# Projections two blocks at a time in the first layer of a four-layer kernel

## The chip, the cores and the metric

The kernel runs on one core of one Trainium2 chip. The metric is device time in microseconds (us) of one execution. A core has a matrix engine (PE; PEld are its weight loads), a vector engine (DVE), a scalar engine (ACT), a general engine (POOL), and a queue (SP) that issues transfers (DMA) between the chip's memory and the on-chip buffers. In the trace of this kernel each engine works off its instructions in the order of its program, and so does SP; they wait for each other through semaphores.

## The reference

The network has four layers on an image batch of 2 x 512 channels x 64 x 64 pixels, all float32. Each layer normalises its input by groups and adds its result to it. Only the first layer matters here. Cut down:

```python
xf = x.reshape(B, C, N).transpose(0, 2, 1)                 # N = 4096 pixels, C = 512
q  = xf @ W_q + b_q                                         # 8 heads of 64 channels
kv = xf @ W_kv + b_kv
k_l, v_l = kv[..., :C], kv[..., C:]
q_norm, k_l = l2norm(q), l2norm(k_l)                        # by head
q_scaled = (q_norm + query_embedding) * softplus(temperature)
# each pixel attends to its 3 x 3 neighbours and to 256 pooled tokens
attn_local = einsum(q_scaled, 9 shifted copies of k_l)
attn_pool  = einsum(q_scaled, l2norm(k_pool))
attn = softmax(concat(attn_local, attn_pool))
lt = einsum(q_norm, learnable_tokens) + learnable_bias + a_local
x_local = sum over 9 neighbours of lt * shifted v_l
x_pool  = a_pool @ v_pool
out = (x_local + x_pool) @ W_proj + b_proj
```

## The kernel before

For each of the two images the four layers run one after the other. The first layer is the class `Local`. It works in 16 units: a unit is one chunk of 128 channels (two heads) by 1,024 pixels, which are two blocks of 512 pixels, `j = 0` and `j = 1`. The loop in `run` is a software pipeline: in the iteration of unit u the following stages run side by side, a step of each in turn (`in_turn`), ten or eleven steps in all:

- `projections`: queries for unit u + 3, keys for u + 4 and values for u + 1. One projection of one block is `project` (L133): four accumulating matmuls of 128 x 128 weights with 128 x 512 data into one PSUM bank. ACT then takes it out of PSUM (L2004 and L2006, with the squares for the norm; L2110 for values).
- `norms` and `normed` (L2036, L2043, the small operations of L2050 to L2058, L2064, L2078, L2086): the l2 norms, of the four streams that the iteration before projected. `learned` is L2099.
- `tap_products` (L2126): DVE multiplies the queries of unit u + 1 with the nine shifted copies of the keys, through three buffers. `tap_sums` (L2139) adds these products up over the channels by matmuls 32 columns wide, two for each neighbour.
- `attend` of unit u: scores against the pooled tokens (L2171, two heads, called four times), exponentials on ACT (L2175), values (L2181), sums of the exponentials on POOL (L2186), denominators (L2193, L2197), their reciprocal on DVE (L2218) and the local weights (L2221, L2222). These weights go to a buffer in memory, `rows` (L2225), from which they are fetched again, spread over 128 partitions, as "taps" (`fetch_tap`, L2235).
- `weigh` of unit u - 1: L2248 and L2251, and then for each of the nine taps two copies on ACT (L2258), two products with the values on DVE (L2261) and one addition on POOL (L2265). A tap is two transfers. There are three tap buffers, so tap k + 3 is fetched after tap k has been added. At the end the sum goes to memory (`yd`, L2271), for the output projection (L1966) that comes later.

The matmuls write to PSUM, of which this stage has eight banks: five that rotate among all of these (`mm`), one for the sums of taps, two for the queries. The code says the order of work only roughly. The tile framework puts the instructions of the whole program in an order of its own for each engine, and the SP queue, when the program is built. The order that it made for PE in a unit of the steady stage, beginning with the denominators, is:

```
L2193 L2197 | project k1 | L2099 | 5 taps | project q0 | 1 tap | project q1 | L2171 |
project v0 | L2036 | L2171 | L2248 | L2043 | L2181 | 4 taps | L2171 | 1 tap | project v1 |
L2171 | 4 taps | L2064 | L2181 | L2078 (k) | 3 taps | project k0 | L2078 (q)
```

A "tap" here is one matmul of L2139, of which a unit has 18. On the SP queue the order of a steady unit is: two transfers to `rows`, four fetches (taps 0 and 1), the one to `yd`, two fetches (tap 2), and later twelve fetches (taps 3 to 8).

The lines with the projections in the step loop are these, before:

```python
for step in range(10):
    if step >= 6:
        project((uk, uq)[step // 2 - 3], "kq"[step // 2 - 3], step % 2)
    if step % 3 == 0 and values:
        u, j = values.pop(0)
        self.value(u, j)
```

Of the kernel before, what the change touches and what calls it, by code (L numbers as in the profile page):

```python
# [1692 lines left out]
class Local:  # L1693
# [300 lines left out]
    def projections(self, uk, uq, uv, streams):  # L1994

        nc = self.nc

        def project(u, which, j):
            if u is None:
                return  # L2000
            b = self.bias[which][:, u // self.UN:][:, :1]
            ps = self.projected(which, u % self.UN * 2 + j)
            part = self.raw[which][:, j * TB:(j + 1) * TB]
            nc.scalar.activation(part, ps, AF.Identity, bias=b)  # L2004
            sq = self.sq[len(streams)]
            nc.scalar.activation(sq, ps, AF.Square, bias=b)  # L2006
            streams.append((which, u, j, part, sq))
            if j and self.last(u):
                self.fetch(which, u // self.UN + 1)

        last = KC * self.UN - 1
        values = [(uv, 0), (uv, 1)] if uv is not None and uv < last - 1 else []
        if uv == last - 1:

            values = [(u, j) for u in (uv, last) for j in range(2)]
        for step in range(10):
            if step >= 6:
                project((uk, uq)[step // 2 - 3], "kq"[step // 2 - 3], step % 2)
            if step % 3 == 0 and values:
                u, j = values.pop(0)  # L2020
                self.value(u, j)
                if j and self.last(u):
                    self.fetch("v", u // self.UN + 1)
            yield

    def norms(self, streams, ended):
# [407 lines left out]
```

## Time and profile before

| | |
|---|---|
| time, median of 3 runs (lowest, highest) | 5502.16 us (5494.62, 5505.77) |
| span of the profiled run | 5486.4 us |
| PE busy | 5213.3 us (95%) |
| PE weight loads busy | 2263.8 us (41%) |
| DVE busy | 3063.3 us (56%) |
| ACT, POOL busy | 1797.6 us, 1802.6 us (33% each) |
| first layer's units, first image | from about 250 to 1,050 us |
| the same, second image | from about 2,990 to 3,790 us |

PE is the busiest engine by far, but the profile warns that busy PE is not PE at its peak, since its matmuls overlap and their ends are modelled. So the starts of groups of matmuls are what is read from it: the distance from one group's start to the next. In the timeline each float32 matmul appears as two records, so a projection of one block is a row "x8".

### The profile page before, as it was taken

To read this page: it belongs to the slowest core of one execution; us is meant where nothing else is said; L and a number is where in the kernel's file an instruction comes from. 1 tells how busy PE (TensorE), PEld (TensorE's weight loads), DVE (VectorE), ACT (ScalarE), POOL (GpSimd) and SP (SyncE) were. 2 spreads that over 40 slices of the span, in tenths; PEclk is the share of its full clock that TensorE was granted. 3 is DMA by queue.
4 is the path that set the end of the run, shared out by engine and by line. 5 is a ranking of instruction groups with operands and counts; after the bars stand their busy time and mean duration, and the time that the engine had idled before them with its cause. 6 is when DMAs were issued, how large, how long until landed. Compare 5 with 4: busy or idle time off the path is not lost. (4 is left out here: it accounts for less than half of the span.)

```text
span 5486.4 us, 51908 instructions
## 1 busy us (share of the span) xinstructions
PE 5213.3 (95%) x19291; PEld 2263.8 (41%) x19291; DVE 3063.3 (56%) x3804; ACT 1797.6 (33%) x3441; POOL 1802.6 (33%) x1198
## 2 busy tenths in 40 slices
PE   7899999999988899999998999999999889999999
PEld 4333333554333444544343333335543334445443
DVE  3256667745679533544432666676456894334444
ACT  1245555233213233222212555542432222332221
POOL 0025555401310145434400355553013001554443
PEclk9899999999989999999998999999999899999999
DMA  3024445500000000100010344455000000000000
GB/s 140 0 65 126 126 124 157 143 18 24 1 2 0 1 1 8 70 24 31 31 53 0 83 125 127 125 152 148 1 24 1 2 0 1 1 8 16 16 16 24
DMA packets 103354, 276.37 MB, mean 50 GB/s; under 512 B 15090, under 2 KB 28146, under 8 KB 101044
## 3 DMA queue, kind: packets, MB, share of 16 engines
q1 hardware_dynamic: 103092, 272.97, 17.2%
q8 instruction: 154, 2.52, 0.2%
q14 instruction: 108, 0.88, 0.1%
HBM read 224.68 MB, written 48.23 MB: 50 GB/s over the span
## 5 line engine op out<-in xcount | busy, mean ns | idle before, releaser
L133 PE MATMUL mm<-big,w 128*128 128x512 f32 x2560 | 1191.1, 610 | 5.2 <-DVE late L2218 5.1
L133 PEld LDWEIGHTS mm<-big,w 128*128 128x128 f32 x2560 | 468.2, 192 | 695.6 <-issue 594.9
L2265 POOL TENSOR_TENSOR late<-late,big 128x1024 f32<-128x1024 f32 x192 | 454.6, 2368 | 300.7 <-DVE big L2261 298.3
L1265 POOL TENSOR_TENSOR total<-prob 128x512 f32<-128x512 f32 x128 | 159.6, 1270 | 758.8 <-ACT prob L1262 758.8
L1617 POOL TENSOR_SCALAR qf_sum<-qf,ksum_ratio 128x512 f32<-128x512 f32 x128 | 198.9, 1562 | 552.6 <-ACT qf L1667 351.3
L1182 PE MATMUL acc<-big,dg 128*128 128x512 f32 x704 | 319.6, 612 | 56.7 <-DVE big L697 25.6
L1438 POOL TENSOR_TENSOR big<-big 128x512 f32<-128x512 f32 x224 | 277.5, 1270 | 235.4 <-ACT big L1429 235.4
L2186 POOL TENSOR_TENSOR late<-late 128x512 f32<-128x512 f32 x128 | 160.6, 1276 | 510.3 <-ACT late L2175 485.0
L1642 DVE RECIPROCAL k<-psD 128x512 f32<-128x512 f32 x64 | 214.9, 3357 | 185.0 <-PE psD L1639 185.0
L697 DVE TENSOR_TENSOR big<-big 128x3968 f32<-128x3968 f32 x72 | 308.8, 4289 | 6.9 <-DVE big L697 0.9
L2261 DVE TENSOR_TENSOR big<-big,mm 128x512 f32<-128x512 f32 x384 | 254.5, 680 | 71.4 <-ACT mm L2258 68.4
L1429 ACT ACTIVATE big<-mm,ed 128x256 f32<-128x256 f32 x512 | 193.7, 488 | 276.7 <-DVE top L1425 249.0
L2258 ACT COPY mm<-big 128x512 f32<-128x512 f32 x384 | 221.3, 594 | 152.3 <-DMA big<-rows 122.2
L1363 PE MATMUL mm<-proj,k 64*128 64x256 f32 x2048 | 265.2, 391 | 0.9 <-ACT k L1330 0.9
L1282 DVE RECIPROCAL recip<-psD 128x512 f32<-128x512 f32 x64 | 214.9, 3358 | 87.1 <-PE psD L1279 87.1
L2126 DVE TENSOR_TENSOR prod<-qs,big 128x1024 f32<-128x1024 f32 x192 | 230.9, 1218 | 44.9 <-PE tap L2139 42.8
L1262 ACT ACTIVATE prob<-mm 128x512 f32<-128x512 f32 x256 | 132.0, 605 | 364.4 <-PE mm L1259 359.2
L1584 DVE TENSOR_REDUCE tops<-mm 128x2 f32<-128x512 f32 x256 | 159.4, 681 | 163.4 <-PE mm L1363 163.3
L1363 PEld LDWEIGHTS mm<-proj,k 64*128 64x128 f32 x2048 | 207.9, 188 | 94.7 <-issue 78.7
L2265 POOL TENSOR_TENSOR late<-late,tap 128x1024 f32<-128x1024 f32 x96 | 226.6, 2360 | 61.0 <-DVE tap L2261 43.6
L1648 PE MATMUL mm<-k,w 128*128 128x512 f32 x512 | 235.6, 602 | 0.0
L1403 PE MATMUL mm<-w,big 128*128 128x512 f32 x512 | 234.5, 602 | 0.0
(369 smaller groups left out, 8387.7 us busy)
## 6 DMA issues: line engine op xcount, KB each, us to landing
big<-rows SPq DMA_DIRECT2D x384, 256.0 KB, 4.0
tap<-rows SPq DMA_DIRECT2D x192, 256.0 KB, 4.2
yd<-late SPq DMA_DIRECT2D x32, 512.0 KB, 4.2
out<-big SPq DMA_DIRECT2D x64, 256.0 KB, 2.0
big<-in_W_kv SPq DMA_DIRECT2D x8, 1024.0 KB, 6.1
rows<-late SPq DMA_DIRECT2D x64, 128.0 KB, 2.4
big<-yd SPq DMA_DIRECT2D x16, 512.0 KB, 4.5
big<-in_x SPq DMA_DIRECT2D x4, 2048.0 KB, 7.6
```

The costliest lines, as they stand in the source:

```text
L133: self.nc.tensor.matmul(ps, w[:, kc, :], X[:, kc, blk * TB:(blk + 1) * TB], start=(kc == 0), stop=(kc == KC - 1))
L697: nc.vector.tensor_tensor(o, a, b, ALU.max)
L1182: nc.tensor.matmul(accs[b], dg, src[:, b * TB:(b + 1) * TB], start=(j == 0), stop=(j == 6))
L1282: nc.vector.reciprocal(r, psD)
L1363: nc.tensor.matmul(pS[h][i][:, t, :], k[lo:lo + HD, tok:tok + P], proj[lo:lo + HD, :], start=True, stop=True)
L1403: nc.tensor.matmul(ps, X[:, kc, lo:lo + P], wv[:, kc, :], start=(kc == 0), stop=(kc == KC - 1))
L1438: nc.gpsimd.tensor_tensor(a, a, part, ALU.add)
L1648: nc.tensor.matmul(ps, self.wo[:, kc, oc * P:(oc + 1) * P], qs[:, kc, :], start=(kc == 0), stop=(kc == KC - 1))
L2126: self.nc.vector.tensor_tensor(self.prods[k % 3].rearrange("p (y x) -> p y x", x=W), qs, self.kx[:, y + dy:y + dy + self.UY, dx:dx + W], A ...
L2258: nc.scalar.copy(ps, part)
L2261: nc.vector.tensor_tensor(part.rearrange("p (y x) -> p y x", x=W), self.vx[:, y:y + self.UY // 2, dx:dx + W], ps.rearrange("p (y x) -> p y ...
L2265: nc.gpsimd.tensor_tensor(out, out, self.taps[k % 3], ALU.add)
```

## The change

Both blocks of a projection are issued in one step: keys in step 6, queries in step 8 and values in step 2 (before, keys in steps 6 and 7, queries in 8 and 9, values in 0 and 3). In the one iteration that projects the values of the last two units, the second pair comes in step 5. The arithmetic, the tiles and the number of instructions stay as they are. Its purpose is that matmuls of one form follow each other on PE and are less often interleaved with narrower ones.

```diff
         for step in range(10):
-            if step >= 6:
-                project((uk, uq)[step // 2 - 3], "kq"[step // 2 - 3], step % 2)
-            if step % 3 == 0 and values:
-                u, j = values.pop(0)
+
+            if step in (6, 8):
+                for j in range(2):
+                    project((uk, uq)[step // 2 - 3], "kq"[step // 2 - 3], j)
+            for u, j in values[:2] if step in (2, 5) else []:
                 self.value(u, j)
                 if j and self.last(u):
                     self.fetch("v", u // self.UN + 1)
+            if step == 2:
+                values = values[2:]
             yield
```

## The prediction

> **What bounds the kernel now.** I read the page first (busy shares), then the table of windows for single units, then PE's timeline inside a unit, then the timelines of DVE, POOL, SP and ACT at the same place. The page says PE; the windows say that in a steady unit PE has no gap:
>
> ```profile
> PE 5213.3 (95%) x19291; PEld 2263.8 (41%) x19291; DVE 3063.3 (56%) x3804; ACT 1797.6 (33%) x3441; POOL 1802.6 (33%) x1198
> ```
>
> ```profile
> 519.66:565.52 45.86, 45.74 (x165) 14.79 (x165) 31.62 (x51) 25.83 (x45) 26.23 (x13) 1.00 0.48 126
> 565.52:611.38 45.86, 45.74 (x166) 14.79 (x165) 31.61 (x51) 25.88 (x45) 26.21 (x13) 1.00 0.47 127
> ```
>
> A unit takes exactly 45.86 us, PE is busy in 45.74 of them, DVE in 31.6, ACT and POOL in 26. What a group costs is the distance between starts in PE's timeline:
>
> ```profile
> 561.89 3.70 PE L133 MATMUL mm<-big,w 128*128 128x512 f32 x8
> 565.52 1.07 PE L2099 MATMUL mm<-qn,big 128*32 128x512 f32 x8
> ...
> 568.21 3.70 PE L133 MATMUL mm<-big,w 128*128 128x512 f32 x8
> 571.84 1.05 PE L2139 MATMUL tap<-prod,cst 128*32 128x512 f32 x2
> 572.82 3.70 PE L133 MATMUL mm<-big,w 128*128 128x512 f32 x8
> 576.45 1.13 PE L2171 MATMUL mm<-big,kp 64*128 64x512 f32 x4
> ```
>
> A projection takes 3.63 us to the next group; its eight passes alone are 3.43 (in the pooled stage, where projections follow each other, the weight loads of passes start 0.429 apart). So 0.20 is a change of form. A single tap matmul (two passes) costs 0.98; four of them that use the four column strips cost 1.00 together (548.83 to 549.83).
>
> Now the loop that PE hides, with L2193 of this unit at 559.02 as zero:
>
> ```profile
> 562.01 3.37 DVE L2218 RECIPROCAL late<-mm 128x256 f32<-128x256 f32 x2 [0.41 <-PE mm L2197]
> ...
> 568.62 0.68 DVE L2261 TENSOR_TENSOR big<-big,mm 128x512 f32<-128x512 f32 x1
> ```
>
> ```profile
> 569.43 2.36 POOL L2265 TENSOR_TENSOR late<-late,big 128x1024 f32<-128x1024 f32 x1 [5.35 <-DVE big L2261]
> 571.87 2.36 POOL L2265 TENSOR_TENSOR late<-late,tap 128x1024 f32<-128x1024 f32 x1
> ```
>
> ```profile
> 567.33 1.11 SPq L2225 DMA_DIRECT2D rows<-late  x2
> 570.37 2.54 SPq L2235 DMA_DIRECT2D big<-rows  x4
> 574.26 0.33 SPq L2271 DMA_DIRECT2D yd<-late  x1
> ```
>
> The reciprocal starts at 2.99, the last-but-one tap is multiplied at 9.6, POOL adds the last two taps until 15.2, and SP, which had fetched taps 0 and 1 of the next unit at 11.4, then writes `yd`. ACT copies tap 0 only at 584.27 (25.25), some 9 us after it landed. This slack makes PE the only bound.
>
> **What the Trainium skill says.** "TensorEngine Tiling (Array Packing)", section "Tiling Modes": a change of tiling mode drains the array, and tiles of one mode run in parallel. The trace agrees: 0.20 us at each change, and four narrow matmuls for the price of one. "TensorE: Matmul & The Clock Gate", section "Measured speedup vs the span model" and the part before it ("Part 3"): matmuls stay in program order; in the trace too, a group whose data is late holds all after it. "DMA: Bandwidth & Descriptors", section "Anatomy of one DMA": waits for semaphores are at the issuing sequencer, before the transfer is handed over. So a transfer that waits on SP holds those behind it; the SP rows above (`yd` issued 0.03 after POOL's end) fit that.
>
> **The change part by part.** I read the new order of each engine from the built program. A steady unit on PE becomes, from the denominators on:
>
> ```
> L2193 L2197 | L2099 | project q0 q1 | L2171 | L2036 | L2171 | L2248 | 5 taps | L2043 | L2181 |
> 4 taps | project v0 v1 | L2171 | 4 taps | L2171 | 3 taps | L2064 | L2181 | L2078 | 2 taps |
> project k0 k1 | L2078
> ```
>
> 1. Projections: six groups of 3.63 = 21.78 become three of 16 passes, 6.86 + 0.20 = 7.06, = 21.18. Saved 0.60.
> 2. Taps: six pieces (0.98 + 0.99 + 0.98 + 1.00 + 0.99 + 1.81 = 6.75) become five (1.81 + 4 x 1.00 = 5.81). Saved 0.94. L2099 no longer shares its form with taps behind it: 0.12 lost.
> 3. L2043 no longer waits 0.18 for ACT after L2248 (five taps lie between). Saved 0.18.
>
> Sum 1.60: PE's own work is 44.25 a unit. Nothing is added on any engine. What moves is the rest: the whole value projection, some 9 us of PE, has gone from before L2248 to behind tap 0, and the loop above must now close sooner.
>
> 4. The new wait. On SP, `yd` now stands in front of all six fetches of taps 0 to 2. On DVE the product that the fourth of the "4 taps" before v0 needs stands behind the two L2261 of tap 0, as it did before. Step by step from L2193 = 0: the reciprocal at 2.99 lasts to 6.36; then L2261, L2221, L2261 at 0.61 each start at 6.39, 7.0, 7.6, so tap 7 goes to POOL at 8.4 (569.43 - 568.62 = 0.8 later), two additions of 2.4 end at 13.2; `yd` is issued at 13.25, the fetches of tap 0 at 13.6 and 14.2. For their landing unit 12 of the first image, where before has `yd` first too, is the nearest row:
>
> ```profile
> 894.19 0.34 SPq L2271 DMA_DIRECT2D yd<-late  x1
> 894.63 0.38 SPq L1956 DMA_DIRECT2D w<-yd  x1
> 895.17 2.63 SPq L2235 DMA_DIRECT2D big<-rows  x4
> ```
>
> ```profile
> 901.94 1.11 ACT L2258 COPY mm<-big 128x512 f32<-128x512 f32 x2 [2.30 <-DMA big<-rows]
> ```
>
> ```profile
> 904.56 2.16 PE L2171 MATMUL mm<-big,kp 64*128 64x512 f32 x4 [1.27 <-DVE big L2261]
> ```
>
> There it was 7.75 us from `yd`, with another 512 KB in between. At the 230 to 250 GB/s that the transfers show there, those take 2.1; so 5.7, landing at 18.9. Lower bound: the quickest tap lands 3.3 after its issue, at 17.5. Upper: 7.75, at 21.0. From landing: copy and two products to 1.9 later, the product of L2126 1.21, PE goes on at 3.3 after landing = 22.2. PE would be there at 19.4 (19.8, since L2036 waits 0.4 for the squares of q1, now right before it). From there PE has 1.0 (taps) + 23.8 left to the next L2193, and about 0.15 behind a copy on ACT that stands behind v1. Unit: 22.2 + 24.95 = 47.15, which is 1.3 longer than 45.86. Behind the held tap matmul on PE stand the values' projections, both score groups and everything to the next L2193, which restarts the loop; so it is not made up.
>
> 5. Number of units: eleven in each image have both this order and a `yd` before them: 2 x 11 x 1.3 = 28.6. Of the 43 changes of form that go in an image, about ten lie in the ramps: -2 us an image, 4 in all. The last units are bound by DVE, POOL and transfers (before already waits in unit 12, rows above), so I take 0 for them. Other layers are untouched. 5502 + 28.6 - 4 = 5527; I say 5525.
>
> **Rivals.** (A) *PE stays the bound, faster.* Tap 0 lands at 17.5 or DVE and POOL get there earlier; then a unit is 44.25 plus 0.4 for the squares and 0.15: 44.8, 1.06 less: 22 x 1.06 + 4 = 27 less, 5475 (without any wait, 5463). For it: PE busy 45.74 of 45.86, the transfers only half busy (0.48). Against: 17.5 needs the least landing of all. (B) *The two cancel*: landing at 17.6 to 18.1 gives 45.8 to 46.3 a unit, about 5500. (C) *Transfers collide as in unit 12*: landing at 21.0, unit 49.3, +3.4: 5502 + 75 - 4 = 5573. For it: `yd` and six fetches, 2 MB, are then queued at once, and the taps behind `yd` before took a median of 6.1 to land. Against: tap 0 needs only the first half of that.
>
> **How the numbers follow.** Forecast (a new wait, 46.4 to 48 a unit, 5510 to 5545) 0.52; C 0.10; B 0.18; A 0.20. Slower by over 0.2% (above 5513): C and nearly all of the forecast, 0.59. Faster (below 5491): A and a little, 0.22. Same: 0.19. The range leaves out the far half of A and C: 5478 to 5558.
>
> **What would show it.** Right: rows of PE with two projections x16 and 7.06 to the next group; five pieces of taps; `yd` on SP ahead of the taps; ACT's copy of tap 0 waiting for DMA in every unit; PE held about 2 us at the taps before v0, for L2126 (L2129 in the new numbering) or L2261; a unit of 47. Wrong: units of 44.3 to 44.8 with PE full, or the hold at another place.

## The result, and the profile after

The changed kernel takes 5539.57 us (median of 4 runs, 5536.88 to 5544.89) against 5498.39 (4 runs, 5482.31 to 5505.77): a ratio of 1.008, 95% interval 1.0056 to 1.0105. It is slower by 41 us.

First the page's line of busy time. The number of instructions on each engine has not changed, and PE's busy time has grown by 23 us:

```profile
PE 5236.5 (94%) x19291; PEld 2281.3 (41%) x19291; DVE 3064.9 (55%) x3804; ACT 1790.9 (32%) x3441; POOL 1811.8 (33%) x1198
```

The windows of two steady units (length, then busy time of PE, weight loads, DVE, ACT, POOL) put a number on what the page blurs. The unit has grown from 45.86 us to 47.3 and 47.6, and PE now has 1.45 and 1.74 us that no matmul fills:

```profile
671.50:718.80 47.30, 45.85 (x168) 15.15 (x166) 31.76 (x50) 25.52 (x46) 26.57 (x13) 1.00 0.47 122
718.80:766.40 47.60, 45.86 (x168) 15.15 (x166) 31.73 (x50) 25.51 (x46) 26.56 (x13) 1.00 0.47 122
```

PE's timeline of the first of them (start, duration; L2196, the first line of a unit, starts at 671.45). Lines of the changed kernel from L2031 on are three higher than before, so L2142 is a tap sum, L2129 its product on DVE, L2238 a tap fetch:

```profile
675.32 7.13 PE L133 MATMUL mm<-big,w 128*128 128x512 f32 x16
682.38 1.13 PE L2174 MATMUL mm<-big,kp 64*128 64x512 f32 x4
683.44 1.41 PE L2039 MATMUL mm<-sq,cst 128*32 128x512 f32 x8
684.78 1.13 PE L2174 MATMUL mm<-big,kp 64*128 64x512 f32 x4
...
686.90 0.62 PE L2142 MATMUL tap<-big,cst 128*32 128x512 f32 x2
...
691.19 0.62 PE L2142 MATMUL tap<-prod,cst 128*32 128x512 f32 x1
691.19 0.62 PE L2142 MATMUL tap<-big,cst 128*32 128x512 f32 x2
...
693.69 1.05 PE L2142 MATMUL tap<-prod,cst 128*32 128x512 f32 x2 [1.45 <-DVE prod L2129]
694.67 7.13 PE L133 MATMUL mm<-big,w 128*128 128x512 f32 x16
```

Read the starts. The two projections take 7.06 (675.32 to 682.38) where two separate ones took 7.26: the saving is there. But the four tap sums that begin at 691.19 end only at 694.67. That is 3.48 for what costs 1.00, so PE is held (it stands at a matmul whose data is not there) for 2.5 us, and the bracket names a product on DVE.

Which sums these are matters for all that follows. DVE makes nine products for a unit, 0 to 8, and writes them into three buffers in turn, which the trace names `big`, `prod`, `prod`. Each product gives two sums, so the 18 sums can be counted by these names. The five from 686.90 on are sums 1 to 5 (product 0 in `big`, product 1, half of product 2). The four at 691.19 are the second sum of product 2, the two of product 3 in `big`, and the first of product 4: sums 6 to 9. Sum 9 is the one that is held. In the kernel before, sums 6 to 9 begin 35.7 us into the unit and product 4 is done at 32.4; now they begin at 19.7 and it is done at 22.2. The build has brought the sums forward by 16 us and the product by 10.

Now the loop behind it, in the timelines of SP, ACT and DVE:

```profile
680.17 1.10 SPq L2228 DMA_DIRECT2D rows<-late  x2
684.87 0.33 SPq L2274 DMA_DIRECT2D yd<-late  x1
685.37 2.43 SPq L2238 DMA_DIRECT2D big<-rows  x4
```

```profile
690.45 1.11 ACT L2261 COPY mm<-big 128x512 f32<-128x512 f32 x2 [3.42 <-DMA big<-rows]
```

```profile
691.12 1.28 DVE L2264 TENSOR_TENSOR big<-big,mm 128x512 f32<-128x512 f32 x2 [1.70 <-ACT mm L2261]
...
692.43 1.21 DVE L2129 TENSOR_TENSOR prod<-qs,big 128x1024 f32<-128x1024 f32 x1
```

Before, ACT came to tap 0 9 us after it had landed. Now it waits 3.42 us for the landing; DVE waits for ACT, the product that PE needs (692.43) stands on DVE behind the two of L2264 for tap 0, and the whole began when SP stood at `yd` until POOL's last addition ended at 684.84. In the nine units of each image from the third on, the hold is 2.4 to 3.8 us, 2.7 in the median.

Where the 41 us are: in each image, the eleven units from the first L2196 to the twelfth take 521.5 and 521.8 us instead of 503.7 and 503.6, 18 more. The ramp from the norm of the pooled tokens to the first L2196 takes 4.5 and 2.4 more, the stretch behind the twelfth 1.7 more and 2.2 less. Together 42. (The two profiled executions themselves differ by 57, 5543.0 against 5486.4: the other 14 lie outside the first layer, which the change does not touch, and the four times of the kernel before alone are spread over 23.)

### The profile page after: what moved, and what is told of

It is laid out like the page before. It is cut to its first block, busy times and chain, and to the rows that moved or that the text cites. A ratio compares the mean times of both kernels' runs of the same rounds, so it can differ in the third digit from the quotient of the medians.

```text
span 5543.0 us, 51933 instructions
## 1 busy us (share of the span) xinstructions
PE 5236.5 (94%) x19291; PEld 2281.3 (41%) x19291; DVE 3064.9 (55%) x3804; ACT 1790.9 (32%) x3441; POOL 1811.8 (33%) x1198
## 5 line engine op out<-in xcount | busy, mean ns | idle before, releaser
L133 PE MATMUL mm<-big,w 128*128 128x512 f32 x2560 | 1168.5, 606 | 1.7 <-DVE big L2264 1.5
L2264 DVE TENSOR_TENSOR big<-big,mm 128x512 f32<-128x512 f32 x384 | 247.3, 676 | 77.8 <-ACT mm L2261 74.8
L2142 PE MATMUL tap<-prod,cst 128*32 128x512 f32 x768 | 221.6, 614 | 34.1 <-DVE prod L2129 24.7
L2129 DVE TENSOR_TENSOR prod<-qs,big 128x1024 f32<-128x1024 f32 x192 | 230.7, 1215 | 40.6 <-PE tap L2142 38.6
L133 PE MATMUL mm<-big,big 128*128 128x512 f32 x512 | 243.2, 638 | 0.0
```

The lines of the kernel that those rows point to most:

```text
L133: self.nc.tensor.matmul(ps, w[:, kc, :], X[:, kc, blk * TB:(blk + 1) * TB], start=(kc == 0), stop=(kc == KC - 1))
L2129: self.nc.vector.tensor_tensor(self.prods[k % 3].rearrange("p (y x) -> p y x", x=W), qs, self.kx[:, y + dy:y + dy + self.UY, dx:dx + W], A ...
L2142: nc.tensor.matmul(ps[32 * q:32 * q + 32, :], self.cst[:, C_TAPW + 16 - 2 * k:C_TAPW + 48 - 2 * k], self.prods[k % 3][:, j * TB:(j + 1) * ...
L2264: nc.vector.tensor_tensor(part.rearrange("p (y x) -> p y x", x=W), self.vx[:, y:y + self.UY // 2, dx:dx + W], ps.rearrange("p (y x) -> p y ...
```

## The experiments

The theory: PE's own work fell as the prediction says, but PE takes its matmuls in order and now reaches tap sums before their products; these stand on DVE behind work on the taps, and that stands behind `yd` on SP. The rivals: two projections of values in a row hold up the other engines; `yd` ahead of the fetches costs by itself, wherever PE stands; PE's early arrival costs, wherever `yd` stands.

The table has what the traces show, in us from the unit's first matmul: which comes first on SP, when the group with sums 6 to 9 begins, when the product for sum 9 is done, and at which sums PE stands for more than 0.2 us until the product is there. Where units differ, the most common kind is given. Ratios are to runs of the kernel before that were made beside each group of runs, with their 95% interval.

| run | first on SP | sums 6 to 9 begin | product for sum 9 done | PE waits at sum | unit, us | time, us | ratio |
|---|---|---|---|---|---|---|---|
| before | taps 0, 1 | 35.7 | 32.4 | none | 45.86 | 5498.39 | 1 |
| after | `yd` | 19.7 | 22.1 to 23.0 | 9, 15 | 47.2 to 47.7 (most) | 5539.57 | 1.008 [1.0056, 1.0105] |
| keys_only | `yd` | 31.2 | 27.9 | none | 44.83 | 5484.61 | 0.9976 [0.9968, 0.9984] |
| all_values_step0 | `yd` | 30.3 | 30.3 | 11, 13, 15, 17 | 51.4 to 53.3 | 5678.50 | 1.0336 [1.031, 1.0362] |
| all_values_step1 | taps 0, 1 | 30.9 | 30.1 | 11 | 46.05 | 5525.15 | 1.0056 [1.0036, 1.0076] |
| all_values_step3 | taps 0, 1 | 22.4 | 24.4 | 7, 9 | 46.95 to 48.0 (most) | 5543.21 | 1.0085 [1.0059, 1.011] |
| yd_on_act_queue | taps 0, 1 | 31.0, 29.6 in turn | 24.3 to 26.6 | none; 11, 15 in turn | 44.83, 46.33 in turn | 5499.00 | 1.0003 [0.9994, 1.0012] |
| values_only | taps 0, 1 | 34.7 | 27.2 | none | 45.01 | 5485.98 | 0.9973 [0.9963, 0.9983] |
| keys_and_queries | taps 0, 1 | 31.0 | 27.7 | none | 44.63 | 5469.00 | 0.9942 [0.9925, 0.9959] |
| half_yd_on_sp | both, see text | 30.8 | 24.4 to 25.6 | none, see text | 44.60 to 47.1 | 5506.81 | 1.001 [1.0, 1.002] |
| keys_queries_yd_act | taps 0, 1 | 31.0 | 27.7 | none | 44.63 | 5460.49 | 0.9926 [0.9907, 0.9946] |
| keys_queries_values_1_3 | taps 0, 1 | 30.8 | 26.6 | none | 44.41 | 5462.80 | 0.993 [0.9911, 0.9949] |
| keys_and_queries_again | taps 0, 1 | 31.0 | 27.7 | none | 44.63 | 5465.05 | 0.9936 [0.9918, 0.9955] |
| best_values_1_3_yd_act | taps 0, 1 | 30.8 | 26.6 | none | 44.41 | 5460.26 | 0.9926 [0.9912, 0.9939] |

The expectations were written by the place of the sums, "the tap sums behind the first pooled values". That is not enough: only in the changed kernel do sums 6 to 9 stand there. In all the other runs the first sums of a series do, and their products were done by 14.3 us, before any tap had landed. What can be compared from run to run is a sum and its own product.

### keys_only: `yd` first, but sums 6 to 9 come later

```diff
-            if step >= 6:
-                project((uk, uq)[step // 2 - 3], "kq"[step // 2 - 3], step % 2)
+            if step == 6:
+                for j in range(2):
+                    project(uk, "k", j)
+            if step >= 8:
+                project(uq, "q", step % 2)
```

> Only the keys are issued side by side (step 6); queries and values stay as before. In the built order yd stands ahead of all six tap fetches, as in the changed kernel, but value block 0 is still projected before L2248, so PE reaches the tap sums behind the first pooled values about 4 us later than in the changed kernel (near 23.7 us after the denominators, against 22.2 for the data). Theory (the loop over yd, tap fetch, ACT, DVE has become later than PE's arrival): no hold, the unit keeps its savings of 0.2 (one change of form) and 0.8 (taps in six pieces of 5.96 instead of 6.76), 44.9 us, total about 5474, 24 less than before. Rival 'yd ahead of the fetches costs by itself, because 2 MB are queued at once': as the changed kernel, about 5540. Rival 'sixteen passes of the values in a row hold up the other engines': 5474 too.

The unit is 44.83 (44.9 was expected), and the run is 13 us faster than before. In this unit L2196 starts at 523.02. SP writes `yd` and issues tap 0 as late as in the changed kernel (13.41 and 13.90 after it; there 13.42 and 13.92):

```profile
536.43 0.33 SPq L2274 DMA_DIRECT2D yd<-late  x1
536.92 2.42 SPq L2238 DMA_DIRECT2D big<-rows  x4
```

In the timelines of DVE and PE:

```profile
549.73 1.21 DVE L2129 TENSOR_TENSOR prod<-qs,big 128x1024 f32<-128x1024 f32 x1
```

```profile
546.51 0.62 PE L2142 MATMUL tap<-big,cst 128*32 128x512 f32 x2
...
554.23 0.62 PE L2142 MATMUL tap<-prod,cst 128*32 128x512 f32 x1
554.24 0.62 PE L2142 MATMUL tap<-big,cst 128*32 128x512 f32 x2
```

The sums at 546.51 begin with product 0: they are sums 1 to 4, and not those that hold the changed kernel, as the expectation took them to be. Sums 6 to 9 begin at 554.23, 31.2 into the unit, and product 4 (549.73) is done 3.3 us before. So `yd` ahead of the fetches costs nothing in a unit whose sums come that late. What it costs where they come early is not shown by this run. The total fell short of the 24 expected: the eleven units gave 10.6 and 9.9 in the two images, and the ramp took 6.4 and 4.6 of that back.

### yd_on_act_queue: nothing in front of the taps

```diff
-        nc.sync.dma_start(self.yd[:, cc, lo:lo + self.UT], out)
+        nc.scalar.dma_start(self.yd[:, cc, lo:lo + self.UT], out)
```

> The changed kernel with yd issued from ACT's queue instead of SP's, so that nothing stands on SP between the writes to rows and the fetches of taps 0 and 1. The built order of PE then alternates between two patterns, with the values' pair still behind the tap sums that follow the first pooled values. Theory (it is yd in front of the fetches that makes the changed kernel's hold of 2.5 us a unit): tap 0 is fetched about 11.4 us after the denominators instead of 13.9, its product is there by 19 to 20 instead of 21.5, and the hold at the first tap sums falls from 2.5 to below 0.5. If nothing else holds PE, the unit is 44.3 to 45 and the total 5460 to 5480; some of it may be lost again to tap sums that follow each other too closely for DVE's three product buffers, as in the run with the values in step 3: then 5490 to 5510. Rival 'PE's early arrival costs whatever stands on SP': hold and time as in the changed kernel, 5540. Rival 'the wait only moves to ACT', which now waits for POOL's last addition before yd: copies late, 5540 or more.

It takes what the kernel before takes: the 41 us are gone. In the unit that starts at 609.76, tap 0 is issued at 11.67 instead of 13.92, and ACT copies it at 16.96 instead of 19.0:

```profile
621.43 2.38 SPq L2238 DMA_DIRECT2D big<-rows  x4
```

```profile
626.72 1.11 ACT L2261 COPY mm<-big 128x512 f32<-128x512 f32 x2
```

```profile
629.41 0.62 PE L2142 MATMUL tap<-big,cst 128*32 128x512 f32 x2
...
631.25 7.13 PE L133 MATMUL mm<-big,w 128*128 128x512 f32 x16
```

Five sums in 1.84 (five cost 1.81): no hold here. But they begin with product 0, so they are sums 1 to 5, whose products were done by 14.1. The move to another queue made the build put sums 6 to 9 at 29.6 and 31.0. Two things have changed at once, the place of `yd` and that of sum 9, and the run does not tell which of them took the hold away.

The trace of the changed kernel gives a bound for the share of `yd`. There DVE had nothing to do for 1.70 us before it took up tap 0 (the bracket at 691.12), so an earlier landing could have brought product 4 forward by 1.70 at most. As an estimate from that line, 1.7 of the hold of 2.5 is due to `yd`, 0.8 would have stayed, and the unit would be 45.6, about as long as before. No run shows this.

The build now alternates between two orders of PE. The units of 44.83 hold 15 tap sums and hardly wait. Those of 46.33 hold 21, in loose pieces (groups that do not run side by side): three sums in 1.29 (641.43 to 642.72), four in 1.74 (646.23 to 647.97), because sums 11 and 15 start only as their products end. That is why the mean, 45.6, is still above 44.8.

### half_yd_on_sp: both orders within one kernel

```diff
-        nc.sync.dma_start(self.yd[:, cc, lo:lo + self.UT], out)
+        mid = lo + self.UT // 2
+        nc.sync.dma_start(self.yd[:, cc, lo:mid], out[:, :self.UT // 2])
+        nc.scalar.dma_start(self.yd[:, cc, mid:lo + self.UT], out[:, self.UT // 2:])
```

> The changed kernel with yd cut in two: half of its columns are written from SP's queue, still in front of the tap fetches, the other half from ACT's. PE reaches the tap sums behind the first pooled values at about 19.9 us after the denominators, as in the changed kernel. Theory (what delays the fetches is that SP stands waiting for POOL's last addition, not the bytes of yd): tap 0 is again issued near 13.9, the hold there stays at 1.7 to 2.5 us, unit 46.3 to 47.2, total 5510 to 5540. Rival 'the bytes of yd in front of the taps delay their landing': half the bytes leave at most half the hold, unit 45.5 or less, total 5500 or less.

The expectation was wrong about the order: the build put the half of `yd` in front of taps 0 and 1 only in units 1, 7, 8 and 9 of an image (counted from 0), and behind them in the others. That makes a better comparison than the one intended. From the start of unit 1 on, the periods in the first image are

```
45.35 | 44.60 44.61 44.76 44.61 45.27 | 47.10 46.08 45.47 | 44.60
```

with bars around units 1 and 7 to 9. SP of unit 5, which starts at 562.05, and of unit 7, which starts at 651.93:

```profile
574.09 2.38 SPq L2238 DMA_DIRECT2D big<-rows  x4
576.56 0.54 SPq L2275 DMA_DIRECT2D yd<-late  x1
```

```profile
665.41 0.33 SPq L2275 DMA_DIRECT2D yd<-late  x1
665.90 2.49 SPq L2238 DMA_DIRECT2D big<-rows  x4
```

Tap 0 is issued at 12.04 in one and 13.97 in the other. The first has all three pairs with the values in step 2, as the changed kernel has, and takes 44.61, because its sums 6 to 9 begin at 30.8: the pairing of all three does not cost by itself. The second takes 47.10, with its sums 6 to 9 at 30.4. Of these 2.5 us, 0.8 stands between its five tap sums and the values' projections (2.60 from start to start for 1.81), which the trace puts down to L2264 of tap 0 (0.69). The rest comes from the build, which gave this unit 20 tap sums for 18 and looser pieces (1.29 for three, 1.74 for four). So the order on SP is seen here in a wait of 0.8, and the rest goes with the order that the build chose.

The bytes of `yd` are not tested by this run, since ACT issued its half in unit 7 at 665.41 too, ahead of tap 0. The landings in the traces answer it. In the changed kernel's units the second transfer of tap 0 lands 4.55 us after its issue, and with `yd` on ACT's queue 4.27 (medians; the first transfer 3.98 and 3.66). The issue is 2.1 later (13.91 against 11.78, medians). So most of the delay is SP's wait for POOL, and 0.3 may be the bytes.

### The values in step 0, 1 or 3

In all three, keys and queries stay paired and the values' pair moves; for step 0:

```diff
-            for u, j in values[:2] if step in (2, 5) else []:
+            for u, j in values[:2] if step in (0, 5) else []:
...
-            if step == 2:
+            if step == 0:
```

> All three pairs side by side as in the changed kernel, but the values in step 0 instead of 2. yd stands ahead of the six tap fetches again; the values' projections (7.06 us) are now ahead of L2248, so PE reaches the tap sums that it was held at about 25 us after the denominators. Theory: no hold; work of PE 21.18 for projections and 5.96 for taps, unit 44.3, total about 5460. Rival 'the pair of values in a row holds up the other engines' and rival 'yd first costs by itself': both stay near the changed kernel, 5540.

> All three pairs side by side, the values in step 1. In the built order taps 0 and 1 are fetched ahead of yd, and the values' projections stand just behind L2248, ahead of the tap sums in question. Theory: nothing can hold PE there (arrival near 27 us, data at 20), unit 44.3, total about 5460. Rival 'the pair of values in a row holds up the other engines': near 5540. Rival 'yd first costs by itself': 5460.

> All three pairs side by side, the values in step 3. Taps 0 and 1 are fetched ahead of yd, but the values' projections stand behind the tap sums in question, as in the changed kernel, so PE reaches those sums at the same early time, about 19.9 us after the denominators. Theory: what decides is when the loop closes; with the fetches issued near 11.4 and landing near 15.6, the sums' products are there near 19, so PE is hardly held: unit 44.3 to 44.9, total 5460 to 5475. Rival 'PE's early arrival alone costs, since nothing lies between L2248 and the sums, with yd first or not': held some 2 us, near 5540. Rival 'the pair of values in a row': 5540.

These three are misses: each is slower than before, the first by 181 us. The sums behind the first pooled values take 1.00 in each, but they are sums 1 to 4 and test nothing. Each build has an order in which later sums come ahead of their products. In the run with step 0, twelve sums (6 to 17) stand in a row behind the scores, starting 30.3 us into the unit, and take 9.8 us instead of 3.0 (three groups of four):

```profile
579.18 3.52 SPq L2238 DMA_DIRECT2D big<-rows  x4
```

```profile
583.88 1.11 ACT L2261 COPY mm<-big 128x512 f32<-128x512 f32 x2 [1.78 <-DMA big<-rows]
```

```profile
585.96 1.21 DVE L2129 TENSOR_TENSOR big<-qs,big 128x1024 f32<-128x1024 f32 x1
```

```profile
583.59 1.05 PE L2142 MATMUL tap<-prod,cst 128*32 128x512 f32 x4 [0.46 <-DVE prod L2129]
587.23 1.92 PE L2142 MATMUL tap<-big,cst 128*32 128x512 f32 x4 [2.59 <-DVE big L2129]
```

This is the same loop one turn later. Tap 3 can only be fetched when POOL has added tap 0 and freed its buffer; it is issued at 579.18 and copied at 583.88. DVE multiplies it, and only then makes the products that PE has been waiting for. (`yd`, which stands first in this run, has no part in it: ACT copied tap 0 23.2 us into the unit, at 574.12, without waiting for it to land.) In the run with step 1, seven sums (6 to 12, from 560.00) take 3.51 for some 1.8. In the run with step 3, five (5 to 9) take 3.02 for 1.81, and the scores ahead of them and a projection behind them lose 0.7 each. Without these waits the units with steps 1 and 3 are 46.05 - 1.7 = 44.35 and 46.95 - 2.6 = 44.35: PE's work fell in both.

With steps 1 and 3 `yd` stands behind taps 0 and 1 and the time still rises, so it has no part in their loss. What the losing orders share is that sums come ahead of their products, at whichever turn of the loop. `yd` in front is one way to make a product late, and in the changed kernel a part of the hold (1.7 by the estimate above).

### values_only and keys_and_queries: which pair can be had

For the values, the last three lines of the change's diff alone; for keys and queries, its first.

> Only the values are issued side by side (step 2); keys and queries stay as before, but the built order puts the two queries next to each other as well. Key block 1 stays behind the denominators, so PE reaches the tap sums behind the first pooled values at about 23.5 us, and taps 0 and 1 stand ahead of yd. Theory: no hold there, work 45.86 - 0.4 (two changes of form) - 0.95 (taps in five pieces) = 44.5, with up to 0.35 for the queries' squares 44.8; total 5465 to 5475. Rival 'two value projections in a row are what costs, wherever PE arrives': near the changed kernel, 5530 to 5540.

> Keys and queries side by side, values as before in steps 0 and 3. Taps 0 and 1 stand ahead of yd, PE arrives at the first tap sums at about 23.5 us, value block 1 stands between the scores. Theory: no hold, work 45.86 - 0.4 - 0.8 = 44.66; total about 5475 (the keys-only run had 44.83 a unit and 13 less than before in all, of which its ramps took back about 10). Rival 'any second pair gathers the tap sums and makes PE wait for DVE's products': 45.9 or more, 5500 or more.

Both are faster than before, so two value projections in a row are not what costs. The values' run missed the 5465 to 5475 that was expected: its unit is 45.01 rather than 44.8, and the stretch behind the twelfth unit takes 4 to 7 us an image more than before. Keys and queries give 44.63 (44.66 was expected) and 5469: 31 faster than the runs of before beside it, and 70 faster than the changed kernel. Here value block 0 stays ahead of the first pooled values and block 1 between the scores, so that PE still comes to sums 6 to 9 3.3 us after the product for sum 9.

### Where nothing waits, nothing is to be gained: the last four

`yd` from ACT's queue, and values in steps 1 and 3, each on top of keys and queries; then both; and keys and queries alone once more.

> Keys and queries side by side (as in the run of that name) and yd issued from ACT's queue. The built orders of PE and DVE in a steady unit are those of the run with yd on SP. Theory: PE reaches the tap sums at 23.5, after their data in both cases, so yd's place is worth nothing: unit 44.63, total as with yd on SP, 5460 to 5475. Rival 'yd on SP costs some 40 us wherever PE stands': 5430 to 5440. Rival 'ACT waiting for POOL before yd holds PE': 5480 or more.

> Keys and queries side by side, values in steps 1 and 3 instead of 0 and 3. Value block 0 then stands behind L2248 and still ahead of the tap sums; tap pieces are the same six, taps 0 and 1 ahead of yd. Theory (only the time at which PE reaches each tap sum counts): unit 44.63 and total 5465 to 5475, as with step 0. Rival 'values behind L2248 cost something by themselves': 45.5 or more, 5485 or more.

> Keys and queries side by side, values in steps 1 and 3, yd from ACT's queue: the two best runs put together. Theory: the steady unit is that of the run with values in steps 1 and 3 (44.41), since neither change removes a hold from the other; total 5450 to 5463, ratio to before 0.991 to 0.993. Rival 'the two add up, since yd on SP still costs something in the last units': 5445 or less. Rival 'ACT waiting for POOL holds the later value projection': 5470 or more.

> The run with keys and queries side by side once more, in five rounds, as the version that beats both kernels: 5469, ratio to before 0.9942, interval within 0.992 to 0.996.

With sums 6 to 9 at 31.0, `yd`'s place is worth nothing that can be seen: the unit is 44.63 with either queue, and the intervals of the ratios overlap widely. Values in steps 1 and 3 bring the unit to 44.41, 0.2 less than expected: value block 0 now stands right ahead of the transposes L2044, and its distance to them is 3.53 and theirs to the next 0.53, against 3.63 and 0.66 where the two are apart. All four ratios lie between 0.9926 and 0.9936 and can't be told apart. A version with keys and queries paired and the values left apart beats both kernels, by 31 to 43 us against the runs of before beside it.

## Why the prediction was right

The direction and the mechanism were right. By its steps:

1. *Projections*: a group of two takes 7.06, as worked out.
2. *Taps*: five pieces, as forecast. One of them, three sums at 704.85, takes 1.29 and not 1.00, because a product on DVE stands behind L2264 there as well.
3. *The sum*: 44.25 a unit was forecast for PE's own work. Taking the hold (2.48) and the wait for the squares (0.34, forecast 0.4) from 47.30 leaves 44.5; the rest of the difference is the 0.3 of point 2. The short units of the experiments (44.60, with all three pairs) agree.
4. *The new wait*: `yd` issued at 13.42 (forecast 13.25), tap 0 copied at 19.0 (landing forecast 18.9), PE there at 19.74 and going on at 22.24 (forecast 19.8 and 22.2), and 25.06 from there to the next unit (forecast 24.95). The chain is read in the trace line by line. That the early place of sum 9 is needed for the hold is shown by the runs whose builds put it back to about 31 and have no other wait: the unit is then 44.4 to 44.8, with `yd` in front (keys_only) or behind. How much of the hold is due to `yd` on SP is only estimated, since no run moved `yd` alone. That nothing behind the hold makes it up is seen in the unit's length.
5. *The size*: 41 came where 24.6 (28.6 less 4) was forecast, near the upper end of the range. Two terms were off, both to the same side. The units gave 18 an image, 1.64 each and not 1.3. The count of eleven was wrong: the forecast order holds in nine, which grew by 1.8 and 1.7 each in the two images. Their hold is 2.7 in the median and not 2.4, and the loose piece of taps of point 2 adds 0.3. The first two units have another order, with 22 and 20 tap sums for 18, and grew by 0.4 to 1.6. And the ramps cost 6.8 in both images together, where I took 4 off. There the changes of form do go, but one more projection, 3.43 us, stands ahead of the first L2196, and DVE's product L2089 is waited for by L2102 (0.84 in each of two units). That projection is moved and not added: one less is left for the units behind the twelfth, which all the same changed by nothing in sum, as taken.

Rival A needed a landing at 17.5; it landed at 19.0. Rival A's unit of 44.8 came only in builds where sum 9 stands later, and not in every build where the taps went first. Rival B's balance failed by the same number. Rival C's collision did not come: the landing took 5.6 from `yd`, close to the 5.7 taken and well under 7.75.

What stays open: why a given step builds one order and not another, since the order is made when the program is built, and what `yd` behind taps 0 and 1 would be worth with PE's order of the changed kernel left as it is.

## What to carry to other kernels

Before work is moved in a pipeline whose first engine is full, write down for each group on that engine when it is reached and when its data is ready. A move that saves work but brings a group forward past that gap buys a wait, and on an engine that works in order everything behind it waits too. Count the members of a group, too: a group at the same place can be another part of the series. Then bring together only what leaves these times alone (here keys and queries, in the builds that these steps gave). A transfer that nobody is waiting for, such as `yd`, is better behind those that somebody is; here that was worth nothing in the build with time to spare (keys_queries_yd_act), and where there is none its worth is estimated and not measured.

## What the runs showed of the hardware

- A write that waits at the head of SP delays the fetches behind it mainly by its wait: tap 0 issued at 13.91 in the changed kernel and at 11.78 in yd_on_act_queue (medians), while from issue to landing its second transfer took 4.55 and 4.27 us.
- Narrow matmuls in different column strips cost 1.00 for four only when the data of all of them is there. Where products came one by one, four took 1.74, seven 3.51 and twelve 9.8 us.
- The same arithmetic in another order of steps moved the steady unit between 44.41 and 53.3 us.
